# Cross-attention of a third layer: running sums before maxima, the last batch's additions on VectorE, and a closing taken in steps

## The chip, the cores and the metric

The kernel runs on one core of one Trainium2 chip. The metric is the device time in microseconds (us) of one execution, as the median of six runs. The profile comes from one further execution.

## The reference, cut to what matters

Four layers follow each other. Each mixes `x` (16 batches of 56 tokens, 256 wide) with a context (16 batches of 1500 rows, 128 wide) by attention. The change touches the cross-attention of the third layer, and the passage from it to the fourth:

```python
# third layer; NH = 16 heads, CHD = 8 wide, no mask over the 1500 rows
ci  = rms_norm(hidden_states, ln_post_cross_w)
cq  = heads(ci @ cq_w, NH, CHD)
ck, cv = jnp.split(encoder_outputs @ ckv_w, 2, axis=-1)
ck, cv = (heads(ck, NH, CHD), heads(cv, NH, CHD))
scores = jnp.einsum('bhqd,bhkd->bhqk', cq / np.sqrt(CHD), ck)
p = jax.nn.softmax(scores, axis=-1)
cctx = jnp.einsum('bhqk,bhkd->bhqd', p, cv)
hidden_states = hidden_states + cctx.reshape(b, l, 128) @ cdense_w
mi = rms_norm(hidden_states, ln_post_attn_w)          # then two gated MLPs
...
# fourth layer
q = layernorm(x) @ Wq * scale
k, v = jnp.split(media @ Wkv, 2, axis=-1)             # 16 heads, 64 wide, masked softmax
```

## The kernel before, in words

The 16 batches form four groups of four. `program` makes a list of 16 items: the four groups in the first layer, the four in the second, and so on. Items 8 to 11 are the third layer, items 12 to 15 the fourth. For each item it runs the attention (`att2` in the third layer, `att13` in the second and fourth), and beside it a generator, `beside(k)`, that holds the work that isn't attention: the part ahead of the next item's attention (`pre13`, `pre2`) and the part behind the previous item's (`post2`, `post13`). The attention takes pieces of that generator with `step()`. What is left when an attention ends is run at once. `then` is the next item's `first`: for the fourth layer that is `first13`, which loads the weights `wl` and makes the absorbed queries `qa` (line 713 for the matmuls, lines 724 and 247 for the copies).

`att2` takes each batch in six turns of its inner loop (here: sixths). One sixth has these parts:

- `weights_pair(b, j)` makes the softmax weights of two chunks of 125 context rows: four small matmuls (L1137) that put the shifts into four PSUM banks, sixteen instructions of score matmuls (L1146), four exponentials on ScalarE (L1151, `pw`). It also adds the weights into `all`, for the denominators: four additions on GpSimd (L1162), two in the first sixth of a batch.
- `largest(ahead, n)` makes scores of a later batch, only for their maxima: four matmuls of 500 columns (eight instructions, L1100), each on its own 32 rows of the array and into a bank of its own, and four reductions on VectorE (L1105).
- `sums_chunk`, twice, multiplies the weights of the sixth before by the values (L1175) into the one bank of `ps_o`. The last of a batch is followed by a copy on ScalarE, a mask on GpSimd (L1186) and a reduction on VectorE (L1189).
- `values` (L1083) or `keys` (L1071, copy L1072) of a later batch, `shifts` once a batch (L1113 to L1126), and `own_sums` once a batch, which sums `all` over the rows (L1201), divides (L1207, L1209), and at a group's end multiplies by `cdense_w` (L1215) and adds to `x` (L1219).
- one `step()` behind `weights_pair`, and one or two at the end of the sixth.

All banks but one come from one pool of seven: `ps_s = ... tc.tile_pool(name="ps_s", bufs=7, space=PSUM)`. The seven go round, so a part may wait for the reader of an older part's bank. The weights `pw` of three sixths have room (pool `pp`, three buffers, shared with the fourth layer's `p`). Each engine executes its instructions in the order in which they stand in its queue. The order in the queues is set by the framework's planner: the order of the program is the priority, and an instruction that the planner takes for ready may stand ahead of one of higher priority.

In the fourth layer `period(u)` runs the attention over blocks of 32 rows: scores (L345), mask and maximum on VectorE (L356, L360), transposes (L367, L379), exponentials (L387), turned blocks (L398), sums (L805), with three `step()` in each period and eight periods in an item.

Of the kernel before, what the change touches and what calls it, by code (L numbers as in the profile page):

```python
# [20 lines left out]
B, N, M = 16, 56, 1500  # L21
D, DM = 256, 128
G = 4
# [38 lines left out]
def tile_kernel(ctx: ExitStack, tc: tile.TileContext, a, layers=4, groups=NG):  # L62
# [3 lines left out]
    nc = tc.nc  # L66
# [13 lines left out]
    def psum(pool, tag):  # L80
        return pool.tile([128, 512], F32, tag=tag, name=tag)
# [5 lines left out]
    def mm():  # L87
        return psum(ps_s, "sc")
# [10 lines left out]
    def tmp(name):  # L99
        return tpool.tile([128, 512], F32, tag="tmp", name=name)  # L100
# [46 lines left out]
    def p_tile(name):  # L147
        return ppool.tile([128, UB * QB], F32, tag="p", name=name)
# [97 lines left out]
    def scalar_copy(out, in_, scale=1.0):  # L246
        nc.scalar.activation(out, in_, AF.Copy, scale=scale)  # L247
# [163 lines left out]
    def step(n=1):  # L411
        for _ in range(n):
            next(line["side"], None)

    line, memory_w, halves_of, queries, heads_w, cross, held = {}, [], {}, {}, {}, {}, {}
# [632 lines left out]
    PAIRS = NC // 2  # L1048
# [42 lines left out]
    def largest(b, n):  # L1091

        made = cross[b]
        s, half = divmod(n, 2)
        rows = slice(half * 2 * N, (half + 1) * 2 * N)
        cols = slice(s * SW, (s + 1) * SW)
        banks = [mm() for _ in range(4)]
        for g in range(4):
            part = slice(g * BW, (g + 1) * BW)
            nc.tensor.matmul(  # L1100
                banks[g][: 2 * N, :SW], made["q"][part, rows], made["k"][part, cols],
                start=True, stop=True,
            )
        for g in range(4):
            nc.vector.tensor_reduce(  # L1105
                made["mx"][:, half * 4 + g, s : s + 1], banks[g][: 2 * N, :SW], AX.X, ALU.max
            )
# [21 lines left out]
    def weights_pair(b, j):  # L1129

        made = cross[b]
        p = p_tile("pw")[:CP, : 2 * R].rearrange("p (c n) -> p c n", c=2)
        made["p", j] = p
        banks = [psum(ps_s, "sc") for _ in range(4)]
        for g in range(4):
            rows = slice(g * BW, g * BW + 2)
            nc.tensor.matmul(  # L1137
                banks[g][:CP, : 2 * QH].rearrange("p (c n) -> p c n", c=2), ones_r[rows],
                made["shift"][rows].unsqueeze(1).to_broadcast([2, 2, QH]),
                start=True, stop=False, skip_group_check=True,  # L1140
            )
        for c in range(2):
            at = (2 * j + c) * CP
            for g in range(4):
                part = slice(g * BW, (g + 1) * BW)
                nc.tensor.matmul(  # L1146
                    banks[g][:CP, c * QH : (c + 1) * QH], made["k"][part, at : at + CP],
                    made["q"][part], start=False, stop=c == 1, skip_group_check=True,
                )
        for g in range(4):  # L1150
            nc.scalar.activation(  # L1151
                p[:, :, g * QH : (g + 1) * QH],
                banks[g][:CP, : 2 * QH].rearrange("p (c n) -> p c n", c=2), AF.Exp,
            )
        if j == 0:
            made["all"] = big.tile([128, 2, H, N], F32, tag="ot", name="all")[:CP, 0].rearrange(
                "p h n -> p (h n)"
            )
        for c in range(0 if j else 1, 2):
            for lo in range(0, R, R // 2):  # L1160
                cols = slice(lo, lo + R // 2)
                nc.gpsimd.tensor_tensor(  # L1162
                    made["all"][:, cols], made["all"][:, cols] if j else p[:, 0, cols],
                    p[:, c, cols], ALU.add,
                )

    def sums_chunk(b, n):

        made = cross[b]
        if n == 0:  # L1170
            made["o"] = psum(ps_o, "o")
        p = made["p", n // 2][:, n % 2]
        for r in range(4):
            part = slice(r * BW, (r + 1) * BW)
            nc.tensor.matmul(  # L1175
                made["o"][part, :QH], made["v"][:, n, part], p[:, r * QH : (r + 1) * QH],
                start=n == 0, stop=n + 1 == NC, skip_group_check=True,
            )
        if n + 1 == NC:
            rest = tmp("rest")  # L1180
            raw, made["own"], made["over"] = (
                rest[:, lo:hi].rearrange("p (h n) -> p h n", n=N)
                for lo, hi in ((0, QH), (QH, QH + N), (QH + N, QH + 2 * N))
            )
            scalar_copy(raw, made["o"][:, :QH].rearrange("p (h n) -> p h n", n=N))
            nc.gpsimd.tensor_tensor(  # L1186
                raw, raw, m_own.unsqueeze(2).to_broadcast([128, 4, N]), ALU.mult
            )
            nc.vector.tensor_reduce(  # L1189
                made["own"][:, 0], raw.rearrange("p h n -> p n h"), AX.X, ALU.add  # L1190
            )
# [48 lines left out]
    def att2(gi, state, then, ends):  # L1240

        for k in range(G):
            b = gi * G + k
            for j in range(PAIRS):
                if k == G - 2 and j == 2 and not ends:
                    then()
                if j == 2 and b + 2 < B:
                    spread_queries(b + 2)
                weights_pair(b, j)
                step()  # L1250
                ahead, n_ahead = divmod(PAIRS * (b + 1) + j + 2, PAIRS)
                if ahead < B:
                    largest(ahead, n_ahead)
                last, n = (b, 2 * j - 2) if j else (b - 1, NC - 2)
                if last >= 0:
                    sums_chunk(last, n)
                    sums_chunk(last, n + 1)
                if j + 2 == PAIRS and b + 1 < B:
                    shifts(b + 1)
                if j == 1 and b:  # L1260
                    own_sums(b - 1)
                if j < NS and b + 1 < B:
                    values(b + 1, j)
                if j >= NS and b + 2 < B:
                    keys(b + 2, j - NS)
                step(2 - j % 2)
        if ends:
            sums_chunk(b, NC - 2)
            sums_chunk(b, NC - 1)
            own_sums(b)  # L1270
            then()

    def post2(gi, state):
        x = xs[gi]
# [46 lines left out]
    def program():  # L1321
        line.update(turn=None, sum=None, side=iter(()), rate=1, closed=0)
        for kept in (memory_w, halves_of, queries, heads_w, cross, held):
            kept.clear()
        load_first()
        parts = [(pre0, first0, att0, post0)]
        for name in ("L1", "L3"):
            parts.append(tuple(partial(f, name) for f in (pre13, first13, att13, post13)))
        parts.insert(2, (pre2, first2, att2, post2))
        items = [(*parts[l], gi) for l in range(layers) for gi in range(groups)]  # L1330
        states = {}

        def run(side):
            for _ in side:
                pass

        def before(k):
            if k + 1 < len(items):
                states[k + 1] = yield from items[k + 1][0](items[k + 1][4])

        def first(k):
            if k < len(items):
                while k not in states:
                    next(line["side"])
                items[k][1](items[k][4], states[k])

        def beside(k):

            if k > groups:
                yield from before(k)  # L1350
            if k:
                while line["closed"] < k:
                    yield
                _, _, _, post, gi = items[k - 1]
                yield from post(gi, states.pop(k - 1))
                if k > len(items) - groups:
                    nc.sync.dma_start(
                        a["out"][gi * T : (gi + 1) * T, :].rearrange("(i p) d -> p i d", p=TP), xs[gi]
                    )
            if k <= groups:  # L1360
                yield from before(k)

        run(before(-1))
        first(0)
        for k, (_, _, att, _, gi) in enumerate(items):
            line.update(side=beside(k), rate=2 if k + 1 == 2 * groups else 1)
            att(gi, states[k], partial(first, k + 1), gi == groups - 1)
            run(line["side"])
        run(beside(len(items)))


# [140 lines left out]
```

## Time and profile before

| | |
|---|---|
| median of 6 runs | 1735.9 us (1734.6 to 1739.15) |
| profiled execution: its own time | 1739.49 us |
| profiled execution: span from first to last instruction | 1737.6 us |
| mean granted TensorE clock | 0.954 |
| busy: TensorE matmul, VectorE, ScalarE, GpSimd | 1567.7, 991.6, 925.3, 462.4 us |
| third layer's attention in the trace | first L1137 at 594.8 us, last L1201 at 1342.5 us |
| fourth layer's first scores (L345) | 1350.89 us |

In the lines of the profile PE is the matmul side of TensorE, PEld its weight loads, DVE VectorE, ACT ScalarE, POOL GpSimd, SP SyncE; L1100 is line 1100 of the kernel. A line of the timeline has start, length (both us), engine, source line, operation, tiles, shapes and count, and in brackets the idle time ahead of it with what ended it. The page also cuts the span into 40 slices of 43.4 us each; a digit is the busy share in tenths.

### The profile page before, as it was taken

The numbers are of one execution on the slowest core, as the hardware profiler recorded it, in microseconds if no ns is written. First come the engines' busy times: TensorE is split into PE (matmuls) and PEld (weight loads), VectorE is DVE, ScalarE is ACT, GpSimd is POOL, SyncE is SP. The second block draws the span as 40 slices with busy tenths as digits, with TensorE's granted clock in tenths as the row PEclk, the third lists the DMA queues.
The fourth block names the chain that finished last, engine by engine and source line by source line (L and its number), as shares of the span: only waits on it lengthen the run. The fifth ranks groups of instructions, "written<-read, shape, count | busy, mean of one in ns | idle before, by whom it ended". The sixth has DMA issues, their size and how long they took to land.

```text
span 1737.6 us, 42075 instructions
## 1 busy us (share of the span) xinstructions
PE 1567.7 (90%) x17768; PEld 1043.0 (60%) x17768; DVE 991.6 (57%) x2086; ACT 925.3 (53%) x2937; POOL 462.4 (27%) x460
## 2 busy tenths in 40 slices
PE   2877899999889888999999999999996899999997
PEld 1656667676566445654556555665653777676665
DVE  1433786666565666465754666456451766675761
ACT  1433787875356124532355324554543777878582
POOL 0000000000000144574444645456468000000000
PEclk9988999999789999999989999999998999999998
DMA  5761212221032102200013001221110123222220
GB/s 153 201 165 70 69 31 67 71 75 42 1 106 71 43 19 67 92 22 19 19 49 116 23 18 51 84 76 35 50 67 10 33 65 116 65 79 64 55 89 8
DMA packets 61576, 111.06 MB, mean 64 GB/s; under 512 B 7534, under 2 KB 45054, under 8 KB 61378
## 3 DMA queue, kind: packets, MB, share of 16 engines
q1 hardware_dynamic: 59994, 102.13, 18.7%
q0 software_dynamic: 864, 4.61, 1.2%
q8 instruction: 142, 2.33, 0.6%
q10 hardware_dynamic: 520, 1.54, 0.3%
q14 instruction: 56, 0.46, 0.1%
HBM read 107.35 MB, written 0.92 MB: 62 GB/s over the span
## 4 chain that ended last, share of the span: by engine, by line
PE 73%; DVE 13%; ACT 6%; DMA 3%; POOL 3%; issue 1%; SPq 0%; POOLq 0%; ACTq 0%; DVEq 0%
PE sc L1100 8%; PE o L805 7%; PE sc L345 7%; PE sc L846 6%; PE sc L1289 4%; PE o L1175 4%; PE sc L1146 3%; PE sc L692 3%; DVE mx L1105 3%; PE sc L1309 3%; PE sc L1083 3%; PE sc L1071 2%; ACT p L387 2%; PE sc L865 2%; POOL all L1162 2%; DVE few L360 2%
## 5 line engine op out<-in xcount | busy, mean ns | idle before, releaser
L1162 POOL TENSOR_TENSOR all<-all,pw 125x448 f32<-125x448 f32 x320 | 362.5, 1144 | 286.6 <-ACT pw L1151 274.8
L1105 DVE TENSOR_REDUCE mx<-sc 112x1 f32<-112x500 f32 x384 | 235.4, 669 | 180.5 <-PE sc L1100 180.2
L387 ACT ACTIVATE p<-p,few 128x96 f32<-128x96 f32 x896 | 322.4, 362 | 2.0
L1151 ACT ACTIVATE pw<-sc 125x448 f32<-125x448 f32 x384 | 178.0, 549 | 149.5 <-PE sc L1146 136.8
L1100 PE MATMUL sc<-ck,qs 32*112 32x500 f32 x768 | 169.5, 624 | 14.3 <-ACT pw L1151 10.3
L805 PE MATMUL o<-p,kvl 128*128 128x448 f32 x384 | 177.7, 573 | 2.5 <-DVE p L398 1.5
L144 POOL TENSOR_SCALAR mkl<-m32l 128x96 bf16<-128x96 uint8 x32 | 8.7, 271 | 621.9 <-issue 319.2
L345 PE MATMUL sc<-ktl,qa 128*32 128x96 f32 x7168 | 168.8, 248 | 4.0 <-issue 2.1
L387 ACT ACTIVATION_READ_ACCUMULATOR p<-p,few 128x1 f32 x896 | 168.8, 188 | 0.0
L345 PEld LDWEIGHTS sc<-ktl,qa 128*32 128x32 f32 x7168 | 151.1, 110 | 20.8 <-issue 10.0
L356 DVE TENSOR_TENSOR p<-sc,mkl 128x480 f32<-128x480 f32 (+1 forms) x192 | 116.3, 613 | 63.3 <-PE sc L345 63.3
L398 DVE STREAM_TRANSPOSE p<-p 128x480 f32<-128x480 f32 (+1 forms) x192 | 116.1, 620 | 12.4 <-ACT p L387 12.2
L360 DVE TENSOR_REDUCE few<-p 128x5 f32<-128x480 f32 (+1 forms) x192 | 117.3, 617 | 5.0
L1175 PE MATMUL o<-pw,vc 125*32 125x224 f32 x1536 | 100.8, 367 | 2.6 <-ACT pw L1151 2.4
L1100 PEld LDWEIGHTS sc<-ck,qs 32*112 32x112 f32 x768 | 57.6, 172 | 72.5 <-ACT pw L1151 44.4
L1175 PEld LDWEIGHTS o<-pw,vc 125*32 125x32 f32 x1536 | 41.8, 110 | 83.7 <-issue 68.2
L1146 PE MATMUL sc<-qs,ck 32*125 32x224 f32 x1536 | 91.4, 351 | 0.0
L805 PEld LDWEIGHTS o<-p,kvl 128*128 128x128 f32 x384 | 65.2, 192 | 41.4 <-issue 28.6
L1289 PE MATMUL sc<-xT,w 128*128 128x224 f32 (+1 forms) x384 | 82.2, 359 | 0.9 <-DVE xT L324 0.9
L748 POOL TENSOR_TENSOR over<-den,tables 32x448 f32<-32x448 f32 x32 | 32.2, 1021 | 173.9 <-DVE den L744 135.6
L247 ACT ACTIVATE vc<-sc 125x512 f32<-125x512 f32 x48 | 28.6, 597 | 91.5 <-PE sc L1083 91.5
L1289 PEld LDWEIGHTS sc<-xT,w 128*128 128x128 f32 (+1 forms) x384 | 65.5, 178 | 17.9 <-issue 6.8
(262 smaller groups left out, 2574.9 us busy)
## 6 DMA issues: line engine op xcount, KB each, us to landing
kt<-in_ctxT SPq DMA_DIRECT2D x23, 750.0 KB
w<-in_L_W SPq DMA_DIRECT2D x16, 1024.0 KB
w<-in_L_Wq SPq DMA_DIRECT2D x8, 1024.0 KB
w<-in_L_Wo SPq DMA_DIRECT2D x8, 1024.0 KB
ktl<-in_ctxT SPq DMA_DIRECT2D x32, 192.0 KB
kvl<-in_ctx_last SPq DMA_DIRECT2D x32, 192.0 KB
w<-in_L_v_qkv SPq DMA_DIRECT2D x4, 768.0 KB
w<-in_L_l_qkv SPq DMA_DIRECT2D x4, 768.0 KB
```

The source lines that it names most:

```text
L345: nc.tensor.matmul(sc[g * BW : (g + 1) * BW, at : at + w], q, k, start=True, stop=True, skip_group_check=True,)
L356: nc.vector.tensor_tensor(p, sc[:, : m * w].rearrange("p (i k) -> p i k", i=m), u["mask"].unsqueeze(1).to_broadcast([128, m, w]), ALU.add,)
L360: return nc.vector.tensor_reduce(u["mx"][:, i : i + m], p, AX.X, ALU.max).ins.name
L387: nc.scalar.activation(u["p"][:, i, : u["w"]], u["p"][:, i, : u["w"]], AF.Exp, bias=u["shift"][:, i : i + 1], accum_out=u["den"][:, i : i ...
L805: nc.tensor.matmul(o[:, : ub * BW], kv[:, j, :], p, start=start, stop=stop)
L1100: nc.tensor.matmul(banks[g][: 2 * N, :SW], made["q"][part, rows], made["k"][part, cols], start=True, stop=True,)
L1105: nc.vector.tensor_reduce(made["mx"][:, half * 4 + g, s : s + 1], banks[g][: 2 * N, :SW], AX.X, ALU.max)
L1146: nc.tensor.matmul(banks[g][:CP, c * QH : (c + 1) * QH], made["k"][part, at : at + CP], made["q"][part], start=False, stop=c == 1, skip_gr ...
L1151: nc.scalar.activation(p[:, :, g * QH : (g + 1) * QH], banks[g][:CP, : 2 * QH].rearrange("p (c n) -> p c n", c=2), AF.Exp,)
L1162: nc.gpsimd.tensor_tensor(made["all"][:, cols], made["all"][:, cols] if j else p[:, 0, cols], p[:, c, cols], ALU.add,)
L1175: nc.tensor.matmul(made["o"][part, :QH], made["v"][:, n, part], p[:, r * QH : (r + 1) * QH], start=n == 0, stop=n + 1 == NC, skip_group_ch ...
L1289: nc.tensor.matmul(p[:w, k * T : (k + 1) * T], wt[:, c, cols], xe[n][:, c, :], start=(c == 0), stop=(c == 1),)
```

## The change

Three edits in the third layer, with no new function but the generator `rest`:

1. In each sixth the two `sums_chunk` calls stand ahead of `largest`.
2. The additions of the weights of the last batch (`b` = 15) are made by VectorE rather than by GpSimd: 22 additions of 125x448.
3. In the last group `then()` is called ahead of the fourth sixth of the last batch rather than after the layer. The last two `sums_chunk` and `own_sums` of the last batch become a generator, `rest`, whose three pieces are the first that item 12's side work takes.

```diff
         for c in range(0 if j else 1, 2):
             for lo in range(0, R, R // 2):
                 cols = slice(lo, lo + R // 2)
-                nc.gpsimd.tensor_tensor(
+                engine = nc.gpsimd if b + 1 < B else nc.vector
+                engine.tensor_tensor(
                     made["all"][:, cols], made["all"][:, cols] if j else p[:, 0, cols],
                     p[:, c, cols], ALU.add,
                 )
...
-                if k == G - 2 and j == 2 and not ends:
+                if (k, j) == ((G - 1, 3) if ends else (G - 2, 2)):
                     then()
                 if j == 2 and b + 2 < B:
                     spread_queries(b + 2)
                 weights_pair(b, j)
                 step()
-                ahead, n_ahead = divmod(PAIRS * (b + 1) + j + 2, PAIRS)
-                if ahead < B:
-                    largest(ahead, n_ahead)
                 last, n = (b, 2 * j - 2) if j else (b - 1, NC - 2)
                 if last >= 0:
                     sums_chunk(last, n)
                     sums_chunk(last, n + 1)
+                ahead, n_ahead = divmod(PAIRS * (b + 1) + j + 2, PAIRS)
+                if ahead < B:
+                    largest(ahead, n_ahead)
...
-        if ends:
+
+        def rest():
             sums_chunk(b, NC - 2)
             sums_chunk(b, NC - 1)
+            yield
+            yield
             own_sums(b)
-            then()
+            yield
+
+        if ends:
+            line["rest"] = rest()
...
         def beside(k):
 
+            yield from line.pop("rest", ())
             if k > groups:
                 yield from before(k)
```

## The prediction

> **What bounds the kernel now.** The page comes first, its slices ahead of the sums.
>
> ```profile
> PE 1567.7 (90%) x17768; PEld 1043.0 (60%) x17768; DVE 991.6 (57%) x2086; ACT 925.3 (53%) x2937; POOL 462.4 (27%) x460
> ...
> PE   2877899999889888999999999999996899999997
> POOL 0000000000000144574444645456468000000000
> ...
> PE 73%; DVE 13%; ACT 6%; DMA 3%; POOL 3%; issue 1%; SPq 0%; POOLq 0%; ACTq 0%; DVEq 0%
> ```
>
> TensorE is the bound, nearly full in the third layer (POOL's digits mark it) but for the two slices at its end, where POOL stands at 6 and 8. Two things are then to be read: what PE does within a sixth, and what it waits for at the end. The timeline of PE in one sixth without side work:
>
> ```profile
> 1284.67 0.47 PE L1137 MATMUL sc<-shift,ones_r 2*125 2x448 f32 x4
> 1284.98 0.93 PE L1146 MATMUL sc<-qs,ck 32*125 32x224 f32 x16
> 1285.74 1.96 PE L1100 MATMUL sc<-ck,qs 32*112 32x500 f32 x8
> 1287.63 0.96 PE L1175 MATMUL o<-pw,vc 125*32 125x224 f32 x16
> 1288.52 1.14 PE L1083 MATMUL sc<-l2w,kt 128*125 128x128 f32 x8
> ```
>
> It looks full, but L1100 takes 1.96 us, where its best is 1.11 (at 1268.78). Weights take four of seven banks, three maxima the others; the fourth maximum waits for the first exponential, and runs alone. The waits of PE's loads in the layer (594 to 1304 us) say so:
>
> ```profile
> PEld sc L1100 <- ACT pw L1151: 44.4, 78, 4.1
> ```
>
> At the end of the layer, in the full timeline (1285 to 1365):
>
> ```profile
> 1316.07 2.23 POOL L1162 TENSOR_TENSOR all<-pw 125x448 f32<-125x448 f32 x2
> ...
> 1318.78 23.00 POOL L1162 TENSOR_TENSOR all<-all,pw 125x448 f32<-125x448 f32 x20
> ...
> 1339.55 0.40 PE L1201 MATMUL sc<-all,l2w 125*32 125x56 f32 x4 [7.87 <-POOL all L1162]
> ...
> 1350.89 2.52 PE L345 MATMUL sc<-ktl,qa 128*32 128x96 f32 x112 [1.92 <-ACT qa L247]
> ```
>
> GpSimd needs 1.15 us for each of the last batch's 22 additions; the closing waits for the last, and `first13` and the fourth layer's scores stand behind the closing. PE has done the last batch's own work by 1331.7.
>
> **Swap, sixths without side work.** No instruction is added; sums need the weights of the sixth before, long done. In the line above they would start at 1285.74 and take 0.89 (L1175 to L1083), to 1286.6. The first exponential (four in 1.85 from 1286.02) is done at 1286.5. So four maxima run together: 1.96 - 1.11 = 0.85 saved. What is late next is the following sixth's weights. The banks go round: weights 4, maxima 4, values 1, so the next weights' last two banks are those of the first two maxima. The first reduction starts 1.12 after L1100 (1268.78 to 1269.90), each takes 0.61 (four in 2.43), so the second is done at 2.34, plus 0.1 (estimate) for the signal. Weights want that bank 1.04 (1238.84 to 1239.88, a maximum that didn't wait) + 1.07 (1288.52 to 1289.59, values) + 0.1 = 2.2 after L1100's start. I charge 0.3: 0.55 net. Windows of L1100's own busy time over the four such stretches (749 to 795, 956 to 993, 1158 to 1194, 1274 to 1304) give 14.05 + 12.08 + 12.09 + 11.74 = 50.0 in 28 calls; 28 x 1.11 = 31.1, so 18.9 could go at most: 22 calls of 0.85. Mine is 22 x 0.55 = 12. Bounds 0 (every gain becomes that wait) and 19. GpSimd covers it just so: 22 additions at 1.16, a mask and a spread of 0.57 each are 26.7 per batch; PE's six sixths, now 30, become 27.
>
> **Swap, sixths with side work.** The same sum over the other four stretches: 31.3 + 30.9 + 31.4 + 14.0 = 107.6 in 60 calls, 41.0 above 60 x 1.11. Not all is to be had. Followed by hand, the sixth at 1246.3 keeps 0.3: its next side step wants the bank that L1298 frees at 1252.9, behind an ACT table load (1.28) and a Silu, which the swap doesn't move. The one at 1254.9 keeps 0.8, since two side steps cover what follows. About half: 18. Bounds: 41, and below nothing -11, from the clock. After a pause of 3.31 us at 873.89, windows show a granted clock of 0.50 until about 888: 10.8 us for 5.4 of work. If the faster PE meets two more such pauses, 11 are lost.
>
> That pause, like two more of 3.31 (684.82, 1077.57), stands between the third and the fourth maximum; with sums ahead of them it would be 3.31 - 0.89 = 2.42. A pause of 2.31 (850.44) left the clock at 1.00, one of 2.35 (1326.32) was followed by 0.57. So a gain from the clock isn't certain and I count none. The Trainium skill ("TensorE: Matmul & The Clock Gate", Part 1) has the clock halved after an idle window of about 3.4 us that runs freely; by that rule the three pauses would mostly be safe after the change, and the estimate 10 us lower. The trace's 2.35 fits only loosely.
>
> **The end.** Start at 1316.68, where PE takes the last batch's third sixth (`own_sums` of batch 14 still waits for GpSimd until there). Before, the fourth layer's first L356 stands at 1352.01, 35.3 later. After, PE has four sixths of 2.06 (1308.53 to 1310.59) and `first13`'s 32 L713 in 2.04 (at 1366.65): 10.3, done by 1327 without waits. VectorE decides: its additions have no row. The nearest are L1017 and L916, 448 columns from SBUF: 0.62 alone, some 0.58 back to back. Queued from 1316.7 are L1189 (behind GpSimd's mask of batch 14), 20 x 0.58 = 11.6 of additions, L1207 and L1209 0.7, four L724 of 0.38 at most: 14.4, to 1331; the last four can't end before the last exponentials (about 1330) by more than they take, so 1332. L356 stands 20 earlier. Behind the waiting L1189 are additions, and behind these L724, so weights of the fourth sixth lose a bank for about 1.5: inside the 1332. The closing isn't gone: L1175 0.9, L1201 0.6, L1215 1.2 of PE in the fourth layer's first period, which has a pause of 2.40 (1353.41) to take some; PE waits there for L1207 and L1209, with the second period's scores behind it. Side work gets three pieces in front: 28 for item 12's 24 places instead of 25, so three more run bare at the item's end. I charge 3 for all this. 20 - 3 = 17.
> Bounds: 22 if the closing hides entirely; 6 if an addition costs VectorE GpSimd's 1.13 (20 x 0.55 = 11 lost). Beside GpSimd's additions VectorE's two-input operations have stretched to 1.56 (L907 at 641.88); but GpSimd has only masks after 1316, so I keep 0.58.
> Free: the `wl` loads, issued at 594.9 already, cost SP's queue nothing when they move; `qa` finds its third buffer empty; GpSimd's mask conversions (L144) stand behind L1186 by priority. Were L1186 behind the one that waits for L356, it would wait one period, within the 6.
>
> **Sum.** 12 + 18 + 17 = 47. Against the profiled execution's 1739.5 (the span of 1737.6 and 1.9 around it): 1692.5. That run lies 3.6 above the median, so 1735.9 - 47 = 1688.9: 1689.
>
> **Rivals.** *The swap only moves the wait*: weights wait for maxima as long as maxima waited for exponentials. For it: seven banks remain, and DVE L1105 now starts later by 0.2 or so. Against it: 18.9 of the gain needs only the second of four reductions. Then the end alone counts: 1719.
> *Slower: the last reduction decides.* If the planner lets other tiles take banks between, weights wait for the fourth: 1.12 + 2.43 = 3.55 after L1100's start, where they could start at 2.11: 1.44 in each of 88 sixths, 127, against 60 saved; with the end's 17 that is +50: 1786. It decides once the mean wait passes (60 + 17) / 88 = 0.87. Against it: in the whole trace PE's loads wait for L1105 6.3 us at L1083 and L1100 together.
> *Nothing changes*: the planner, which already sets L1113 (at 1272.37) ahead of maxima that the program has first (1276.62), keeps PE's order, and the end loses its gain to slow additions and pauses: 1736.
>
> **Chances and range.** The forecast (1664 to 1711) 0.70, moved wait 0.18, slower 0.08, nothing 0.04. The low end takes 72 of gain: 19 + 33 + 20, not all upper bounds at once. The high end reaches 1724, over the moved wait with 12 at the end. A measurement of this kernel can tell about 0.2%, 3.5 us, from no change. Faster 0.70 + 0.18 = 0.88, same 0.04, slower 0.08.
>
> **What would show it.** Right: L1100 near 115 us busy rather than 169.5, its wait for L1151 below 10; L1137 waiting for L1105 by some 0.3 in quiet sixths; in the timeline DVE L1162 x22 at 0.6, GpSimd's last L1162 at the end of batch 14, and L345 of the fourth layer some 20 us after the third sixth of the last batch, with no pause above 3 us. Wrong: a wait of L1137 for L1105 above 0.85 a sixth; more windows at a clock of 0.5; L1201 of the last batch waiting for DVE.

## The result and the profile after

The changed kernel takes 1747.7 us (median of 20 runs, 1739.0 to 1751.1) against 1735.9 for the kernel before in the same sessions (46 runs): a ratio of 1.0058, interval 1.0048 to 1.0068. It is slower by 0.6%, 10 us, where 47 us less had been forecast. Behind the edits most lines of `sums_chunk` and `own_sums` have moved by one: additions L1163, sums L1176, GpSimd's mask L1187, VectorE's reduction of the masked sums L1190, closing L1202, L1208, L1210, L1216. L1137, L1146, L1151, L1100 and L1105 are where they were.

The page of the profiled execution (its own time 1742.99 us, span 1741.2, mean granted clock 0.943 against 0.954 before): busy times, slices, the chain that ended last, and one group.

```profile
PE 1571.5 (90%) x17768; PEld 1036.4 (60%) x17768; DVE 1000.4 (57%) x2108; ACT 927.2 (53%) x2939; POOL 438.8 (25%) x438
...
PE   3887899999879899998989989899998899999997
...
PEclk9999999999888889998889998899998999999998
...
PE 67%; DVE 15%; ACT 7%; POOL 5%; DMA 4%; issue 1%; SPq 0%; POOLq 0%; ACTq 0%; DVEq 0%
...
L1100 PE MATMUL sc<-ck,qs 32*112 32x500 f32 x768 | 132.5, 658 | 10.2 <-ACT pw L1151 8.2
```

What the swap set out to do, it did: L1100 is busy 132.5 us rather than 169.5 (the prediction had some 115). In the two slices at the layer's end (the 31st and 32nd) the 6 and 8 of before have become 8 and 8. But the slices ahead of them show many more 8s, PEclk has 8s in the same stretches, and on the chain PE gives up six points while VectorE and GpSimd win four: something runs from GpSimd over VectorE to TensorE.

The waits of the layer (589 to 1352 us) name it. The columns are total, number and longest.

```profile
DVE rest L1190 <- POOL rest L1187: 50.0, 15, 4.8
PEld sc L1137 <- DVE mx L1105: 23.7, 54, 2.1
PE sc L1137 <- DVE mx L1105: 8.8, 6, 1.8
PE sc L1296 <- DVE xT L324: 8.4, 3, 3.6
```

In the kernel before, from 590 to 1310 us, VectorE's reduction waits 5.7 us in 9 places, and L1137 has no row for L1105. (Its last two reductions come later and wait 11.8 and 22.3 us for GpSimd's additions of the last two batches, at a point where no maxima are left to make.)

```profile
DVE rest L1189 <- POOL rest L1186: 5.7, 9, 0.8
```

Fifteen waits, one per batch. The timeline of the changed kernel around one of them, the first sixth of batch 4:

```profile
781.23 1.11 PE L1100 MATMUL sc<-ck,qs 32*112 32x500 f32 x8
781.99 2.23 POOL L1163 TENSOR_TENSOR all<-pw 125x448 f32<-125x448 f32 x2
782.03 0.39 ACT L247 ACTIVATE rest<-o 128x224 f32<-128x224 f32 x1
...
784.18 0.56 POOL L1187 TENSOR_TENSOR rest<-rest,tables 128x224 f32<-128x224 f32 x1
784.77 0.53 DVE L1190 TENSOR_REDUCE rest<-rest 128x56 f32<-128x224 f32 x1 [3.90 <-POOL rest L1187]
785.22 2.43 DVE L1105 TENSOR_REDUCE mx<-sc 112x1 f32<-112x500 f32 x4
...
785.95 1.90 PE L1137 MATMUL sc<-shift,ones_r 2*125 2x448 f32 x3 [1.76 <-DVE mx L1105]
...
789.27 3.69 PE L970 MATMUL sc<-w,xT 128*112 128x512 f32 x4
```

And VectorE at the same place before the change:

```profile
782.11 2.43 DVE L1105 TENSOR_REDUCE mx<-sc 112x1 f32<-112x500 f32 x4 [1.31 <-PE sc L1100]
785.30 0.56 DVE L1189 TENSOR_REDUCE rest<-rest 128x56 f32<-128x224 f32 x1 [0.77 <-POOL rest L1186]
```

In the first sixth of a batch the sums that the swap puts in front are the last of the batch before, and only these bring a closing: copy on ScalarE, mask on GpSimd, reduction on VectorE. The mask stands behind the new batch's two additions (781.99 to 784.18). The reduction waits for the mask, and now stands ahead of the four maxima in VectorE's queue. The first maximum's scores are ready at 782.3 (1.12 after 781.23, the distance that the prediction measured), and their reduction begins at 785.22, 2.9 late. Four banks are held that long; the next weights get one L1137 done and then wait 1.76. After that pause TensorE runs at half the clock. The windows of that stretch (columns: window, its length and PE busy, then the granted clock):

```profile
784.00:785.90 1.90, 0.18 (x1) 1.00 0.00 0
785.90:789.30 3.40, 3.35 (x20) 0.51 0.00 0
789.30:793.00 3.70, 3.70 (x9) 0.53 0.00 0
793.00:797.00 4.00, 3.69 (x64) 1.00 0.02 4
```

L970, 1.97 us before the change, takes 3.69 in it. Banks are not the only way: the two longest pauses of this kind, 3.5 us each (ahead of 905.76 and of 1113.88), are side work (L1296) that waits for VectorE's L324, which stands behind the late maxima in the same queue (the row of L1296 above).

Taking the sixths of batches 1 to 14 from one L1137 to the next, in the two traces: the first two sixths lost 31.6 us in 28 places, all but 3.9 of it where there is side work, and the other four won 8.8 in 55. From the layer's first weights to the last batch's third sixth, where the end begins, the changed kernel takes 746.8 us instead of 721.9.

### The profile page after: what moved, and what is told of

Its sections match the earlier page's. It is cut to its first block, busy times and chain, and to the rows that moved or that the text cites. A ratio compares the mean times of both kernels' runs of the same rounds, so it can differ in the third digit from the quotient of the medians.

```text
span 1741.2 us, 42081 instructions
## 1 busy us (share of the span) xinstructions
PE 1571.5 (90%) x17768; PEld 1036.4 (60%) x17768; DVE 1000.4 (57%) x2108; ACT 927.2 (53%) x2939; POOL 438.8 (25%) x438
## 4 chain that ended last, share of the span: by engine, by line
PE 67%; DVE 15%; ACT 7%; POOL 5%; DMA 4%; issue 1%; SPq 0%; POOLq 0%; ACTq 0%; DVEq 0%
PE o L805 7%; PE sc L345 6%; PE sc L846 6%; PE sc L1100 5%; PE sc L1296 5%; DVE mx L1105 4%; POOL all L1163 4%; PE sc L1146 3%; PE o L1176 3%; PE sc L692 3%; ACT p L387 2%; PE sc L1316 2%; PE sc L1137 2%; DVE few L360 2%; PE sc L865 2%; PE sc L1004 2%
## 5 line engine op out<-in xcount | busy, mean ns | idle before, releaser
L1163 POOL TENSOR_TENSOR all<-all,pw 125x448 f32<-125x448 f32 x300 | 340.4, 1147 | 317.2 <-ACT pw L1151 306.0
L1105 DVE TENSOR_REDUCE mx<-sc 112x1 f32<-112x500 f32 x384 | 235.3, 669 | 202.2 <-PE sc L1100 202.2
L1151 ACT ACTIVATE pw<-sc 125x448 f32<-125x448 f32 x384 | 177.9, 548 | 170.7 <-PE sc L1146 166.3
L345 PEld LDWEIGHTS sc<-ktl,qa 128*32 128x32 f32 x7168 | 151.7, 111 | 18.3 <-issue 10.5
L356 DVE TENSOR_TENSOR p<-sc,mkl 128x480 f32<-128x480 f32 (+1 forms) x192 | 116.4, 613 | 62.5 <-PE sc L345 62.5
L1100 PE MATMUL sc<-ck,qs 32*112 32x500 f32 x768 | 132.5, 658 | 10.2 <-ACT pw L1151 8.2
L1146 PE MATMUL sc<-qs,ck 32*125 32x224 f32 x1536 | 107.5, 374 | 0.0
L1176 PE MATMUL o<-pw,vc 125*32 125x224 f32 x1536 | 100.8, 372 | 0.2 <-ACT rest L247 0.2
L1296 PE MATMUL sc<-xT,w 128*128 128x224 f32 (+1 forms) x384 | 85.6, 370 | 8.4 <-DVE xT L324 8.4
L1146 PEld LDWEIGHTS sc<-qs,ck 32*125 32x125 f32 x1536 | 83.3, 197 | 2.1
L1296 PEld LDWEIGHTS sc<-xT,w 128*128 128x128 f32 (+1 forms) x384 | 68.7, 186 | 26.5 <-DVE xT L324 10.3
L1137 PE MATMUL sc<-shift,ones_r 2*125 2x448 f32 x384 | 69.6, 497 | 12.1 <-DVE mx L1105 8.8
```

What stands on the lines that cost most here:

```text
L345: nc.tensor.matmul(sc[g * BW : (g + 1) * BW, at : at + w], q, k, start=True, stop=True, skip_group_check=True,)
L356: nc.vector.tensor_tensor(p, sc[:, : m * w].rearrange("p (i k) -> p i k", i=m), u["mask"].unsqueeze(1).to_broadcast([128, m, w]), ALU.add,)
L1100: nc.tensor.matmul(banks[g][: 2 * N, :SW], made["q"][part, rows], made["k"][part, cols], start=True, stop=True,)
L1105: nc.vector.tensor_reduce(made["mx"][:, half * 4 + g, s : s + 1], banks[g][: 2 * N, :SW], AX.X, ALU.max)
L1146: nc.tensor.matmul(banks[g][:CP, c * QH : (c + 1) * QH], made["k"][part, at : at + CP], made["q"][part], start=False, stop=c == 1, skip_gr ...
L1151: nc.scalar.activation(p[:, :, g * QH : (g + 1) * QH], banks[g][:CP, : 2 * QH].rearrange("p (c n) -> p c n", c=2), AF.Exp,)
```

## Experiments

Theory Q: VectorE's queue. The reduction that waits for GpSimd's mask stands ahead of the maxima once a batch, and the clock makes more of that pause. Rival B: the swap itself; TensorE reaches its banks sooner than VectorE can free them, in every sixth. A minor one, E: the end's two edits cost more than they bring. Differences in us below are ratios times 1735.9, against the runs of the kernel before beside them.

**The swap alone** (edit 1 of the diff, nothing else).

> The kernel before with only the first edit: sums in front of maxima in each sixth. The additions of the last batch stay on GpSimd, the closing stays at the layer's end. If the end edits gain what the two traces show (18 us to the fourth layer's first mask, less 3 behind it), this is slower than the changed kernel by about 15: 1763, range 1757 to 1770. Both theories Q and B say so; a rival in which the end edits do the harm would have it below 1736.

1756.1 us, ratio 1.0111 (1.0092 to 1.0129): +19, at the low edge of what was expected.

**The end alone** (edits 2 and 3, maxima first as before).

> The kernel before with the second and third edit only (last batch's additions on VectorE, closing in steps, early then); maxima stay in front of sums. Theories Q and B: 1736 - 15 = 1721, range 1715 to 1727. Rival (the end edits do the harm, the swap is harmless): 1745 or more.

1722.3, ratio 0.9917 (0.9895 to 0.994): -14. So E falls, and what is lost is lost by the swap.

**The swap in the first sixth alone.**

```diff
-                if ahead < B:
+                if j and ahead < B:
                     largest(ahead, n_ahead)
...
                     sums_chunk(last, n + 1)
+                if not j and ahead < B:
+                    largest(ahead, n_ahead)
```

> The kernel before with the sums in front of the maxima only in the first sixth of each batch, where the sums are the last of the batch before and bring the copy, the mask and the reduction with them; five sixths of six as before, no other edit. Theory Q: nearly all of the harm is here: 1736 + 28 = 1764, range 1752 to 1770, VectorE's wait for GpSimd's mask near 50 us in the layer. Theory B: a sixth of the harm at most, 1736 + 5 = 1741, and the other sixths hold the rest.

1779.2, ratio 1.0249 (1.0225 to 1.0274): +43, more than the whole swap and above the range given. The waits of its third layer:

```profile
DVE rest L1189 <- POOL rest L1186: 54.6, 13, 5.6
PEld sc L1137 <- DVE mx L1105: 15.4, 22, 2.0
PE sc L1137 <- DVE mx L1105: 7.8, 5, 1.7
```

One sixth in six holds the whole harm; if the parts add up, the swap in the other five is worth 43 - 19 = 24. Rival B can't say that. But it doesn't yet show that the reduction's place is what harms.

**The closing issued behind the maxima** (all three edits; copy, mask and reduction become a function of their own).

```diff
+                if last >= 0 and not j:
+                    masked_sums(last)
```

behind `largest`, where `masked_sums` holds the three instructions that followed the last `sums_chunk`.

> The changed kernel with all three edits; only the copy, mask and reduction that follow a batch's last sums (ScalarE L247, GpSimd L1187, VectorE L1190 of the changed kernel) are issued behind the maxima of that sixth rather than with the sums. Theory Q (VectorE's queue: the reduction of the masked sums waits for GpSimd, and now stands ahead of the four maxima): the sixths that begin a batch lost 32 us in the changed kernel's trace (j = 0 and 1 together, over 15 batches); these come back, 1748 - 32 = 1716, range 1705 to 1725, the waits of VectorE for GpSimd's mask fall from 50 us to below 10, and the waits of L1137 for L1105 from 32 to below 20. Theory B (banks: maxima that start behind the sums hold the next weights' banks in every sixth): nothing but 0 to 5 us comes back, above 1740.

1735.6, ratio 1.0001 (0.9986 to 1.0015): a miss, 10 below the changed kernel and not 32. Its waits say why:

```profile
DVE rest L1193 <- POOL rest L1190: 45.7, 14, 4.9
```

The edit did only a little of what it was for: in the instruction order of VectorE, 11 of the 14 reductions of the first sixths still stand ahead of all four maxima, and the other three (at 655.0, 849.6 and 1055.0) stand between them. The planner puts forward what it takes for ready. The run alone speaks neither for Q nor against it.

**The reduction tied behind the maxima** (as before, and an ordering dependency, without a semaphore, from the reduction to the last maximum).

```diff
+        if behind:
+            tc.add_manual_dep(
+                own.ins, behind,
+                mybir.DependencyInfo(
+                    mybir.DependencyClass.NoSync, mybir.DependencyReason.DATA
+                ),
+                reason="maxima go first",
+            )
```

> All three edits; in the first sixth of a batch the closing of the batch before (ScalarE's copy, GpSimd's mask, VectorE's reduction of the masked sums) is issued behind the four maxima, and VectorE's reduction is tied behind the last of them, so that it can't stand ahead of them in VectorE's queue; sums stay in front of the maxima. Theory Q (the reduction that waits for GpSimd holds up the maxima): 1716 (1705 to 1725), 32 below the changed kernel; waits of VectorE's reduction for GpSimd's mask fall from 50 us to below 10, waits of the weights' matmuls (L1137) for the maxima from 33 us to below 15. Rival B (TensorE runs faster into banks that are free no sooner, whatever VectorE's order is): 1740 or more, and the weights' waits for maxima stay above 25 us.

1701.0, ratio 0.9798 (0.9775 to 0.9821): 35 faster than before the change, 45 faster than the change. Against the last run only the dependency is new, and it brings 35 of the 45. The waits of its layer (L1138 is its weights' shift matmul, L1191 and L1194 its mask and reduction), and the same place as above in its timeline:

```profile
PEld sc L1138 <- DVE mx L1105: 9.7, 40, 0.7
...
DVE rest L1194 <- POOL rest L1191: 1.5, 1, 1.5
```

```profile
774.10 2.43 DVE L1105 TENSOR_REDUCE mx<-sc 112x1 f32<-112x500 f32 x4 [1.47 <-PE sc L1100]
...
775.47 1.00 PE L1138 MATMUL sc<-shift,ones_r 2*125 2x448 f32 x4
...
776.51 0.53 DVE L1194 TENSOR_REDUCE rest<-rest 128x56 f32<-128x224 f32 x1
...
777.46 1.97 PE L970 MATMUL sc<-w,xT 128*112 128x512 f32 x4 [0.23 <-DVE xT L324]
```

Maxima at once, no pause, L970 at full clock, and the reduction doesn't wait, since by its turn the mask is there. This settles Q against B. The gain passes Q's own range; two more rows show what it is made of. From the layer's first L1137 to the last batch's third sixth, the changed kernel and this one:

```profile
589.20:1335.90 746.70, 695.18 (x6490) 0.94 0.15 49
```

```profile
590.40:1294.20 703.80, 665.00 (x6496) 0.98 0.16 52
```

42.9 us apart: 30.2 are the same matmuls taking longer and 12.7 idle time. The clock accounts for the first: 746.7 x 0.06 - 703.8 x 0.02 = 31 of full-speed time lost. It cost more than twice what the waiting did. But not all of it stands directly behind the waits. In the changed kernel seven pauses of 1.5 to 3.6 us in which TensorE waits for VectorE's late maxima or L324 (ending at 753.19, 785.95, 905.76, 995.09, 1113.88, 1203.27 and 1307.11) are each followed by a clock of 0.50 to 0.71 for the next 3 to 7 us, some 13 of the 31. Much of the rest follows pauses that both kernels have: behind three of 1.77 us at L992 (ending at 614.23, 812.63 and 1020.74) the next 4 us have 0.62, 0.59 and 0.60; behind the same three in the tied kernel, and in the kernel before, they have 1.00. Why these were slower here, no run tells.

**The mask ahead of the additions** (the changed kernel, with GpSimd's two additions of the first sixth issued behind the mask and tied there; the reduction stays ahead of the maxima).

> The changed kernel, with GpSimd's two additions of a batch's first sixth issued behind the masking of the last batch's sums and tied behind it; VectorE's reduction stays ahead of the maxima. At one such place (782) the masking would start when ScalarE's copy ends (782.42) instead of at 784.18, so the reduction ends about 1.75 earlier and the maxima start 1.2 late instead of 2.9 late. Theory Q: most of the 47 that tying the reduction behind the maxima gained comes this way too, 1716 (1705 to 1730), and the reduction's waits for GpSimd fall from 50 us to below 28. If the two additions aren't what it waits for (the copy is): 1740 or more.

1716.8, ratio 0.9890 (0.9858 to 0.9921), as forecast; the reduction's waits fell less than expected, to 36.3, but the weights' no longer have one of 1.7:

```profile
DVE rest L1206 <- POOL rest L1202: 36.3, 15, 4.8
PEld sc L1137 <- DVE mx L1105: 15.0, 52, 0.8
```

The second way of shortening the same chain, from the other end, wins back 29 of the 45. The row counts VectorE's idle time from its last instruction, also where no scores are ready yet. Counted from when they are ready (1.12 after L1100 starts), the maxima of 14 first sixths begin 29.6 us late in the changed kernel, 13.6 here and 1.8 in the tied kernel: the two additions ahead of the mask are more than half of the wait.

**The swap in five sixths** (edits 2 and 3, `largest` first when `j` is 0).

> Edits to the additions and to the closing as they are; the sums stand in front of the maxima in five sixths of a batch, but behind them in the first, as before the change. Theory Q: the five sixths' swap is worth what the difference of two runs gives (the swap alone +20, the first sixth alone +43: -23), on top of the two other edits' 1722: 1700 (1692 to 1712). Rival B (the swap by itself costs, and the first sixth is only its worst place): 1735 or more.

1707.9, ratio 0.9827 (0.9807 to 0.9847): -30, in the range for Q. On top of the end's 14 the five sixths bring 16, not the 24 of the difference above: the parts don't simply add up. With the wait out of the way the swap may be good in the first sixth too, 1701.0 against 1707.9, but the two intervals overlap.

**The end's two edits apart.** Additions on VectorE, with the closing in its old place; then the closing in steps, with GpSimd's additions.

> The kernel before, with the last batch's additions on VectorE as the only edit: the closing still stands ahead of the fourth layer. By the prediction's steps the additions end at about 1332 instead of 1342 or so and the last closing's matmuls wait until then: some 7 us of the 7.87 pause go, 1729 (1725 to 1732). If the gain is all in the closing's place: 1736.

> The kernel before, with the closing in steps beside the fourth layer (and its item's start) as the only edit: GpSimd still adds, until about 1342, but the fourth layer's scores don't wait for it. If the place is what counts: nearly the whole gain of both edits together (13.5), 1724 (1720 to 1730). If the fourth layer's first period waits for the late closing all the same: 1732 or more.

1720.9, ratio 0.9916 (0.9886 to 0.9946), and 1731.3, ratio 0.9973 (0.9955 to 0.9991): -15 and -5, against -14 for both; the first is below its range, the second near the case in which the fourth layer waits all the same. The additions give the whole gain. The closing's new place gives nothing more that these runs can tell once VectorE adds: in the traces it has L356 15.7 after the last batch's third sixth instead of 20.9, but the fourth layer then takes 391.2 from there on instead of 384.8. With GpSimd adding, the new place mostly moves the wait, and the fourth layer shows the same fault in its own queue:

```profile
1330.41 0.66 DVE L356 TENSOR_TENSOR p<-sc,mkl 128x480 f32<-128x480 f32 x1 [9.22 <-POOL all L1163]
...
1337.30 0.40 PE L1202 MATMUL sc<-all,l2w 125*32 125x56 f32 x4 [2.73 <-POOL all L1163]
...
1340.09 0.53 DVE L1190 TENSOR_REDUCE rest<-rest 128x56 f32<-128x224 f32 x1 [6.04 <-POOL rest L1187]
...
1340.54 0.27 DVE L369 TENSOR_REDUCE nm<-sc 14x32 f32<-14x128 f32 x1
```

The fourth layer's L369 stands behind a reduction that waits for GpSimd, and TensorE's L1202 waits in front of the second scores.

**The fifth sixth.** In the tied kernel it takes 5.53 on average without side work, 4.78 before the change, while the other sixths without side work became shorter on average. Of the five, three are 0.38 longer, one is 0.62 shorter, and that of batch 14 is 3.24 longer (2.81 to 6.05). Its `shifts` have TensorE (L1121) wait for VectorE's subtraction (L1117), which the sums used to cover (in batch 14 the wait is 2.10, against 0.16 in the kernel with the end's edits alone). Three tries: the shifts ahead of the maxima, in the tied kernel and in the one with five sixths, and the fifth sixth in its old order.

```diff
+                if j + 2 == PAIRS and b + 1 < B:
+                    shifts(b + 1)
                 behind = largest(ahead, n_ahead) if ahead < B else None
...
-                if j + 2 == PAIRS and b + 1 < B:
-                    shifts(b + 1)
```

> As the kernel with the tied reduction, and the shifts of the next batch (TensorE's transposes of them wait for VectorE's subtraction, which is queued behind maxima) go ahead of the maxima in the fifth sixth. If those shifts cost what the fifth quiet sixths show (5.7 us instead of 5.3, in some 15 batches), 6 less than that kernel: 1710 (1700 to 1722). If their wait is hidden by other work: no change from it, 1716.

> As the kernel with the swap in five sixths, and in the fifth sixth the shifts of the next batch go ahead of the maxima. If the shifts' wait for VectorE costs some 0.4 in each of 15 batches, 6 less: 1694 (1685 to 1706); if it is hidden, 1700.

> The kernel with the reduction tied behind the maxima, with the maxima first again in the fifth sixth of a batch, whose shifts wait for VectorE. In the profile of the tied kernel that sixth takes 5.53 without side work against 4.78 before (five such), and 10.21 with side work against 10.72 before (nine such): -3.8 and +4.6, so no difference: 1701 (1694 to 1707). If the shifts' wait slows the sixths behind as well: 1692.

1709.5, 1718.7 and 1710.9; ratios 0.9854 (0.9826 to 0.9881), 0.9883 (0.9859 to 0.9906), 0.9858 (0.9828 to 0.9889). All three are misses, 8 to 11 slower than the kernels they start from. For the first the timeline shows a part of it:

```profile
962.33 0.96 PE L1177 MATMUL o<-pw,vc 125*32 125x224 f32 x16
963.01 0.67 DVE L1116 CAST minus<-few 112x8 fp32r<-112x8 f32 x1
963.71 1.05 DVE L1117 TENSOR_TENSOR minus<-few,minus 112x8 f32<-112x8 f32 x1
964.82 0.59 PE L1121 MATMUL sc<-ident,minus 112*32 112x112 f32 x16 [1.52 <-DVE minus L1117]
965.34 1.11 PE L1100 MATMUL sc<-ck,qs 32*112 32x500 f32 x8
```

With the maxima behind the shifts, nothing covers VectorE's chain, and L1121 holds L1100 up for 1.52; with the maxima in front, they covered about one. Three such sixths without side work are 0.95 longer each, some 3 in all; the rest is not traced to a place. For the third, 3.24 of the 3.8 that its forecast hoped to win lie in batch 14, whose fifth sixth makes no maxima: the edit doesn't touch it (6.06 and 6.05). In its trace the fifth sixths of batches 1, 5 and 9, which have side work, are 1.9 to 2.7 longer than in the tied kernel, 6.8 of the 8.9 by which the two spans differ. So the swap helps there; what makes those three differ from the rest stays open. The tied kernel, 1701.0, has the lowest median of all versions.

## Why the prediction was wrong, step by step

**What bounds the kernel** held: TensorE is the bound, L1100 ran alone behind exponentials, and the end waited for GpSimd's additions.

**Swap.** The step that failed is the sentence that the swap needs nothing but weights of the sixth before, "long done". That is true of the matmuls. It is not true of what `sums_chunk` issues with the last of a batch: copy, mask and reduction, on three other queues. The prediction followed TensorE's row alone. The very sixth that it shows, from 1284.67, is the first of a batch (batch 14, the last but one), and VectorE's row of the same place has the reduction waiting for the mask, behind the maxima as yet:

```profile
1289.85 0.55 DVE L1189 TENSOR_REDUCE rest<-rest 128x56 f32<-128x224 f32 x1 [0.64 <-POOL rest L1186]
```

It did not ask where that reduction would stand in VectorE's queue once the sums go first. It even had the pattern in hand at the end ("behind the waiting L1189 are additions") and did not look for it where the swap put it. Price: 45 us by the tied kernel, so +10 in place of -35; that is 45 of the 57 us between forecast and result. The rest is sizes.

**Its size without that.** The tied kernel shows what the swap's own two terms were worth: 18.3 in its trace from the layer's first weights to the last batch's third sixth, 21 by the ratios (0.9917 to 0.9798), where 12 + 18 = 30 were charged. The quiet sixths: 22 of them gain 0.44 each (0.55 forecast), but the five fifth sixths lose 3.8 in all, nearly all of it in one, which was not seen: together 6.0, not 12. Those with side work: 12.3, not 18. The weights' wait for a maximum, 0.3 in the forecast, is 9.7 us over 40, 0.24 each. (The 0.1 that it took for a signal was an estimate without a row; at 785.95 above, the load starts 0.06 after the end of the reduction that it waits for.)

**The clock.** No gain was counted for the three pauses of 3.31. In the tied kernel they are 2.74 (ending at 683.56, 868.09 and 1063.36), and the windows of the 11 us behind them have 0.84 each, where before the change they have 0.76, 0.53 and 0.84: at 11 x (0.87 - 0.48), some 4 us are won. A step that wasn't made is the other sign: short pauses also cost clock, 0.51 after 1.76, and the layer's clock up to the last batch's third sixth fell from 0.97 to 0.94, a sign that the prediction had named for being wrong. Its pause of 2.31 at 850.44, after which the clock stayed at 1.00, is a misreading: TensorE is busy there without a gap (3.70 us of 3.70, 849.00 to 852.70). The pauses of 1.77 at L992 in the kernel before show what it was meant to show. The Trainium skill ("TensorE: Matmul & The Clock Gate", Part 1) gives an idle window of about 3.4 us, running freely; the pause of 1.76 is half of that and was enough here, so the page's number is no safe length for a single pause; nor did every pause of that length cost clock.

**The end** held. L356 stands 35.3 us after the last batch's third sixth before, 17.1 after (1335.92 to 1353.02): 18.2 gained, 20 forecast, and the fourth layer is 2.6 longer, 3 charged. With the 24.8 that the layer lost before that, the two traces give +9, near the +10 measured. The runs give 14 for the 17. What was wrong is whose it is: the additions alone bring it, and the early `then` and the closing in steps add nothing that the runs can tell. An addition costs 0.62 (four in 2.48 at 1318.80 of the end's kernel), not 0.58.

**The rivals.** The slower one had the right outcome in kind, maxima that end too late for the next weights, but by tiles that the planner lets in between, in all 88 sixths at 1.44. Its test, a mean wait of 0.87 a sixth, would have acquitted this trace: the loads of L1137 wait 23.7 us for maxima, 0.27 in each of 88 sixths. Fifteen waits of VectorE, seven of them with a pause of TensorE and a slow clock behind, did what an average of 0.27 doesn't show. The prediction gives its high end as 1711 and then as 1724, which don't agree; 1747.7 lies above both.

## What to carry to other kernels

Before a block is moved ahead of another, list all that it issues, on every queue and in every turn of its loop, the first and the last above all; an instruction that waits for a slow engine (here GpSimd's two additions and a mask) must not stand in front of work that frees banks. Program order may not be enough for that: read the order of the instructions, and tie it where it matters. Price a pause of TensorE with the clock behind it: here the slow matmuls cost more than twice the waiting, though not all of them stood behind the waits that the change made.

## What the runs showed of the hardware

- A pause of 1.76 us (784.19 to 785.95) with the clock at 1.00 was followed by 7 us at 0.51 to 0.53. A pause of 1.77 us in the kernel before (ending at 618.84) was followed by 4 us at 1.00. So the length of a pause alone did not set its price here.
- VectorE's additions take 0.62 alone and 1.30 each beside GpSimd's, in the kernel with only the additions moved, and GpSimd's 1.24 instead of 1.15:

```profile
1303.08 8.69 POOL L1163 TENSOR_TENSOR all<-all,pw 125x448 f32<-125x448 f32 x7
1305.90 2.60 DVE L1163 TENSOR_TENSOR all<-pw 125x448 f32<-125x448 f32 x2 [3.86 <-ACT pw L1151]
```

  The Trainium skill ("SBUF — State Buffer", "Who interferes with whom") states that a VectorE operation with two SBUF inputs contends with a GpSimd operation that reads SBUF; this row agrees, and shows that GpSimd pays less than VectorE. So the bound of the prediction, 1.13 for an addition, was real, but only for two of the 22.
- A subtraction of 112x8 on VectorE (L1117) took 1.05 at 963.71, while GpSimd added without a break (956.70 to 968.25); the same one took 0.17 at 972.90 in the kernel before, where GpSimd added without a break as well (969.40 to 974.07). So GpSimd's being busy doesn't explain it; what does wasn't tried.
